# A mixture-of-experts layer on one core: the first tiles' table moved ahead of other TensorE work, and weight columns gathered a step earlier

## The chip, the cores and the metric

The kernel runs on one core of a Trainium2 chip. A core has five engines that run side by side, each with its own instruction queue in program order: PE (TensorE, matmuls and transposes; its weight loads are listed as PEld), DVE (VectorE), ACT (ScalarE), POOL (GpSimd, which here issues the indirect transfers) and SP (SyncE, which issues plain transfers). They wait for each other through semaphores. Transfers run on DMA engines beside them. The metric is the device time of one execution in microseconds (us), the median of several runs; lower is better.

## The reference

4096 tokens of 256 values, 64 groups of 64 tokens. A gate picks two of eight experts for each token; each expert is a network of three layers (256 to 512 to 512 to 256). The two experts' outputs are weighted by the gate's softmax and added to the token.

```python
var = jnp.mean(x * x, axis=-1, keepdims=True)
xn = rms_w * (x * jax.lax.rsqrt(var + EPS))
gate = xn @ wg_W + wg_b + (genre_embed @ gg_W + gg_b)
gate_w = jax.nn.softmax(gate, axis=-1)
topk_w, topk_i = jax.lax.top_k(gate_w, TOP_K)          # TOP_K = 2
cw = jnp.sum(jax.nn.one_hot(topk_i, E, dtype=x.dtype) * topk_w[..., None], axis=-2)
h1 = jax.nn.relu(jnp.einsum('bsh,ehm->bsem', x, W1) + b1)
h2 = jax.nn.relu(jnp.einsum('bsem,emn->bsen', h1, W2) + b2)
out_e = jnp.einsum('bsen,enh->bseh', h2, W3) + b3
x = x + jnp.einsum('bseh,bse->bsh', out_e, cw)
```

## The kernel before

Only the chosen experts are computed. Tokens are sorted by expert into tiles of 128 rows (`BT`), each of one expert, and 67 such tiles run in this profile. The first eight (`E`) are special: the first 1024 tokens (`NA = 8` columns of 128, "part A") are routed ahead of the rest, and each expert gets one tile of them, so that matmuls can begin while the other 3072 tokens ("part B") are still being routed.

**The head.** `first_part` loads x, transposes it on PE (`turn`, L184: four transposes of a block into one PSUM bank and one copy to SBUF, on ACT or DVE), multiplies the transposed blocks with the gate weights (`gates`, L194, gates lie in rows of 32 per block), and turns the gates upright again (`upright`, L205: one ACT copy and four transposes). `squares` (L177) sums the squares of one column of tokens on ACT or DVE. For part A, `choose` (L252) finds the two largest gates: for each of the two, a maximum (L271), a compare (L275), and then a product with `rank`, a maximum and a compare (L277, L279, L281) that keep the first among equal gates. `count` (L287) makes running counts of the tokens of each expert, `totals` (L300) sums over partitions with four small matmuls on PE, `pick` (L306) gives each token its place in its expert's tile, a compare (L406) makes a one-hot of the places, and 16 matmuls (L424) turn the one-hot into a table of token numbers, from which L426 and L427 make `idxA`, the row numbers that POOL gathers by. `busy` (L214) puts transposes of the identity on PE as filler. In this part the code stands in a `manual_schedule` block: every engine executes in program order.

**The tiles.** `gather(b)` (L587) fetches the 128 token rows of tile b by an indirect transfer on POOL; `gather_cw(b)` (L591) fetches the rows of gate weights ("weight columns") of those tokens in the same way, into a ring `cg` of three buffers. `transpose_x(b)` (L606) brings the rows into matmul layout: for tiles under 12 with PE transposes (L618) and a DVE copy (L620), later through a DRAM scratch and a DVE transpose (L609). `stage_1`, `stage_2` and `stage_3` copy the weights of the tile's expert on DVE into fixed places (L646, L654, L665) for tiles from 8 on; `stage_3` also copies the expert's weight column out of `cg` (L668) and scales the bias with it (L670). `layer1`, `layer2`, `layer3` are the matmuls (L680, L693, L705) with ReLU on ACT (L683, L696). At the end DVE forms `y` (L706) and POOL adds it to the output with an indirect accumulating transfer (L707); each add waits for the one before it. For tiles under 8, L670 and L706 read `cg` itself and not a copy.

**The order.** A step s runs layer 1 of tile s, layer 2 of tile s-1 and layer 3 of tile s-2. `head_step` (tiles 0 to 6) lays pieces of the routing of part B (`rest`, L457 on) between the matmuls, by budgets in ns that `routing` and the generator's `yield`s count. Steps 8 to 59 stand outside of `manual_schedule`: there a planner orders each engine's instructions by when their inputs would be ready. The last steps and the tail (one of 14 branches, by how many tiles there are) are in program order again. Weights of all experts (16 MB) are loaded by SP behind x, in the order of the experts, until about 65 us.

Of the kernel before, what the change touches and what calls it, by code (L numbers as in the profile page):

```python
# [9 lines left out]
F32 = mybir.dt.float32  # L10
# [3 lines left out]
ALU = mybir.AluOpType  # L14
# [7 lines left out]
def kernel(  # L22
# [31 lines left out]
    NA = 8  # L54
# [59 lines left out]
    make_identity(nc, ident)  # L114
    ones = const.tile([P, P], F32, name="ones")
    nc.gpsimd.memset(ones, 1.0)
    rank = const.tile([P, E], F32, name="rank")
    nc.gpsimd.iota(rank, [[-1, E]], base=E, channel_multiplier=0, allow_small_or_imprecise_dtypes=True)
    tri = const.tile([P, P], F32, name="tri")
    nc.gpsimd.affine_select(  # L120
        out=tri, in_=ones, pattern=[[1, P]], compare_op=ALU.is_gt, fill=0.0, base=0, channel_multiplier=-1
# [4 lines left out]
    segA = const.tile([P, E, NA], F32, name="segA")  # L126
    nc.gpsimd.memset(segA, 1.0)
    nc.gpsimd.memset(segA[:, :, 0:1], 0.0)
    iotx = const.tile([P, P, GC], F16, name="iotx")
    nc.gpsimd.iota(iotx, [[1, P], [0, GC]], base=0, channel_multiplier=0, allow_small_or_imprecise_dtypes=True)  # L130
    iot = const.tile([P, NREST], F32, name="iot")
# [25 lines left out]
    def t2(name, n, dt=F32):  # L157
        return buf(gx, [P, n], name, dt)
# [18 lines left out]
    def squares(i, eng):  # L177
        xi = xin[i // TPB][:, i % TPB, :]
        if eng == "A":
            nc.scalar.activation(sqs[eng], xi, AF.Square, accum_out=ss[:, i : i + 1])  # L180
        else:
            V.tensor_tensor_reduce(sqs[eng], xi, xi, 1.0, 0.0, ALU.mult, ALU.add, ss[:, i : i + 1])

    def turn(j, c, n, eng):  # L184

        tp, xTc = TB[n], hid[:, n].rearrange("p c t -> p (c t)")
        for k in range(TPB):
            nc.tensor.transpose(tp[:, ts(k, P)], xin[j][:, k, ts(c, P)], ident)
        if eng == "V":
            V.tensor_copy(xTc, tp)  # L190
        else:
            nc.scalar.copy(xTc, tp)

    def gates(c, bufs, bank=PB[3]):  # L194

        for q, n in enumerate(bufs):
            nc.tensor.matmul(
                bank[32 * q : 32 * q + 32, :],
                lhsT=wg_sb[:, c, :],
                rhs=hid[:, n].rearrange("p c t -> p (c t)"),  # L200
                start=(c == 0),
                stop=(c == HC - 1),
            )

    def upright(nq, bank=PB[3], dst=PB[4]):  # L205

        R = 32 * nq
        nc.scalar.copy(gTs[0:R, :], bank[0:R, :])
        gtp = dst[:, 0 : TPB * R].rearrange("p (k r) -> p k r", k=TPB)
        for k in range(TPB):  # L210
            nc.tensor.transpose(gtp[:, k], gTs[0:R, ts(k, P)], ident[0:R, 0:R])
        return gtp.rearrange("p k (q e) -> p q k e", q=nq)[:, :, :, 0:E]

    def busy(n):  # L214

        for _ in range(n):
            nc.tensor.transpose(PB[6][:, 256 : 256 + P], ident, ident)

    class Part:


        def __init__(self, z, i0, i1):
            self.i0, self.i1, self.n, self.z = i0, i1, i1 - i0, z
            n = self.n
            self.t = {a: t2(f"{a}{z}", n) for a in ("var", "root", "y", "t", "rstd", "m1", "m2", "top", "den", "d2")}
            self.gate, self.w = t3(f"gate{z}", n), t3(f"w{z}", n)
            self.oh, self.pr = (buf(gx, [P, TOPK, n, E], f"{a}{z}") for a in ("oh", "pr"))
            self.inc = buf(gx, [P, E, n], f"inc{z}")
            self.seg = segA if z == "A" else seg
            self.off = PB[6][:, 448 : 448 + 2 * E].rearrange("p (a e) -> p a e", a=2)  # L230
            self.cw8 = cw8B[:, i0:i1, :] if z == "B" else t3("cw8A", n)
# [19 lines left out]

        def choose(self, raw):  # L252

            m1, m2, top = (self.t[a] for a in ("m1", "m2", "top"))
            gate, left, rstd = self.gate, self.pr[:, 0], self.t["rstd"]
            if raw is None:
                V.tensor_tensor(gate, graw[:, self.i0 : self.i1, :], self.over_e(rstd), ALU.mult)
            else:
                q = raw.shape[1]
                V.tensor_tensor(  # L260
                    gate.rearrange("p (q k) e -> p q k e", q=q),
                    raw,
                    self.over_e(rstd).rearrange("p (q k) e -> p q k e", q=q),
                    ALU.mult,
                )
            yield
            V.tensor_tensor(gate, gate, self.over_i(ggate), ALU.add)
            yield
            for k, (g, m) in enumerate(((gate, m1), (left, m2))):
                sc = self.oh[:, k]  # L270
                V.tensor_reduce(m, g, AX.X, ALU.max)  # L271
                yield
                if k == 0:
                    nc.gpsimd.tensor_tensor(self.w, gate, self.over_e(m1), ALU.subtract)
                V.tensor_tensor(sc, g, self.over_e(m), ALU.is_equal)  # L275
                yield
                V.tensor_tensor(sc, sc, self.over_i(rank), ALU.mult)  # L277
                yield
                V.tensor_reduce(top, sc, AX.X, ALU.max)  # L279
                yield  # L280
                V.tensor_tensor(sc, sc, self.over_e(top), ALU.is_equal)  # L281
                yield
                if k == 0:
                    V.scalar_tensor_tensor(left, sc, -BIG, gate, ALU.mult, ALU.add)
                    yield
# [58 lines left out]
    def first_part():  # L344
# [25 lines left out]
        for i in range(TPB):  # L370
            squares(TPB + i, "VVAA"[i])
        V.tensor_copy(ggate, gps)
        gates(0, (0, 2))
        gates(1, (1, 3))
        pA.root()
        pA.norm()
        raw = upright(GA)
# [9 lines left out]
            load_weights(e)  # L387


        for q in range(4):  # L390
            turn(GA + q, 0, q, "A")
        gates(0, range(4))
        squares(NA, "A")
        squares(NA + 1, "A")
        for _ in pA.choose(raw):
            pass
        pA.count()
        for q in range(2):
            turn(GA + q, 1, q, "A")
        pA.totals()  # L400
        slot = pA.gate
        V.scalar_tensor_tensor(
            slot, pA.inc.rearrange("p e i -> p i e"), -1.0, pA.over_i(pA.off[:, 0, :]), ALU.add, ALU.add
        )
        pA.pick(lo16A.rearrange("p (k i) -> p k i", k=TOPK), slot)
        V.tensor_tensor(ohA, iotx, lo16A.unsqueeze(1).to_broadcast([P, P, GC]), ALU.is_equal)  # L406
        V.tensor_tensor(
            mvA.rearrange("p (k i) e -> p k i e", k=TOPK),
            pA.oh,
            toka.unsqueeze(1).unsqueeze(3).to_broadcast([P, TOPK, NA, E]),  # L410
            ALU.mult,
        )
        V.tensor_copy(totA, pA.off[:, 1, :])
        for q in range(2, 4):
            turn(GA + q, 1, q, "A")
        squares(NA + 2, "A")
        gates(1, range(4))
        raw = upright(4)
        nc.scalar.copy(graw[:, NA : NA + 4 * TPB, :].rearrange("p (q k) e -> p q k e", q=4), raw)
        squares(NA + 3, "A")  # L420
        squares(NA + 4, "A")
        tabA = PB[7][:, 0:E]
        for g in range(GC):
            nc.tensor.matmul(tabA, lhsT=ohA[:, :, g], rhs=mvA[:, g, :], start=(g == 0), stop=(g == GC - 1))  # L424

        V.tensor_scalar(sa[:, 0:E], tabA, 0.0, float(NT), ALU.is_equal, ALU.mult)  # L426
        V.scalar_tensor_tensor(idxA, tabA, float(OFFA), sa[:, 0:E], ALU.add, ALU.add)  # L427

    def second_part():

        j0 = GA + 4
        for i in range(NA + 8, NI - 4):
            squares(i, "V")
        for c in range(HC):
            for q in range(2):
                turn(j0 + q, c, 2 * c + q, "A")
        for c in range(HC):
            gates(c, (2 * c, 2 * c + 1), PB[7])
        busy(4)
        raw = upright(2, PB[7], PB[6])  # L440
        busy(2)
        nc.scalar.copy(graw[:, j0 * TPB : NI, :].rearrange("p (q k) e -> p q k e", q=2), raw)
        vps = PB[6][:, 384 : 384 + 2 * E * MC]
        nc.tensor.transpose(vps, vecs, ident[: 2 * E * MC, : 2 * E * MC])
        V.tensor_copy(vT.rearrange("p l e c -> p (l e c)"), vps)
        for i in range(NA + 5, NA + 8):
            squares(i, "A")

    mms = []

# [310 lines left out]
    def step(s, last):  # L761
# [26 lines left out]
        if not ends:  # L788
            layer3(s - 2)
            if s < last:  # L790
                stage_3(s - 1)
        if s < last:
            gather_cw(s)

    SURE = E + NSURE
    CUT = SURE - 2
# [5 lines left out]
    V.tensor_copy(tok16, tokv)  # L802

    with tc.manual_schedule():
        first_part()
        for b in range(3):
            gather(b)
        second_part()
        for i in range(NI - 4, NI):
            squares(i, "V")  # L810
        other = rest()

        def routing(ns):
            while ns > 0:
                c = next(other, None)
                if c is None:
                    break
                ns -= c

        busy(18)  # L820
        routing(100)
        stage_1(0)
        transpose_x(0)
        for s in range(E - 1):
            head_step(s, routing)
        for _ in other:
            pass
        step(E - 1, SURE)
# [59 lines left out]
```

## Time and profile before

| | us |
|---|---|
| median of 3 runs | 530.45 (530.05 to 531.66) |
| the profiled execution | 530.45 |
| its span, first to last instruction | 528.6 |
| PE busy in the span | 510.9 (97%) |
| DVE, ACT, POOL busy | 285.5, 215.4, 282.1 |
| mean granted TensorE clock | 0.993 |
| first layer-1 matmul (tile 0) | at 32.03 |
| layer 1 of tile 1 | at 34.85 |
| from layer 1 of one tile to the next, from tile 12 on | 7.09 |

Times in the profile count from the first instruction. The execution's time is 1.85 us longer than the span. A row of the timeline gives start, duration, engine, line of the kernel, operation, and tiles as out<-in; in brackets stands how long the engine was idle before, and what the profile takes for the release. Names have lost their buffer numbers, so that all `cg` look alike. A busy PE is not PE at its peak[...].

### The profile page before, as it was taken

How to read it: one execution, taken by the hardware profiler on the slowest of the kernel's cores; microseconds unless marked ns; L12 is line 12 of the kernel's file. 1: busy time of each engine (PE TensorE's matmuls, PEld its weight loads, DVE VectorE, ACT ScalarE, POOL GpSimd, SP SyncE). 2: the span in 40 equal slices, each digit the busy share in tenths (PEclk: the TensorE clock that was granted, in tenths of full speed). 3: DMA queues.
4: the chain of work that ended last, by engine and by line, in shares of the span. 5: the costliest groups of instructions: out<-in, count | busy, mean ns of one | idle time of the engine just before them, and what ended most of it. 6: DMA issues, size and time to landing. Idle time of an engine off the chain costs nothing. (4 is left out here: it accounts for less than half of the span.)

```text
span 528.6 us, 11667 instructions
## 1 busy us (share of the span) xinstructions
PE 510.9 (97%) x4026; PEld 487.6 (92%) x4026; DVE 285.5 (54%) x651; ACT 215.4 (41%) x588; POOL 282.1 (53%) x237
## 2 busy tenths in 40 slices
PE   8989999989999999999999999999999999999992
PEld 6579999979999999999999999999999999999991
DVE  4686973347555555555555555555555555545540
ACT  3754334433443444444334444443444444344430
POOL 4132678677875555555555555555555553245441
PEclk9999999999999999999999999999999999999997
DMA  8999976335444333334333332334333323323211
GB/s 262 385 397 377 373 203 181 70 89 104 97 86 82 68 72 75 71 74 76 78 72 79 70 75 66 80 72 82 71 72 76 73 66 51 52 35 75 29 22 22
DMA packets 67230, 58.92 MB, mean 111 GB/s; under 512 B 38721, under 2 KB 58130, under 8 KB 66900
## 3 DMA queue, kind: packets, MB, share of 16 engines
q1 hardware_dynamic: 51312, 40.69, 24.2%
q0 software_dynamic: 15136, 17.32, 20.1%
q8 instruction: 34, 0.56, 0.4%
q14 instruction: 40, 0.33, 0.2%
q10 hardware_dynamic: 708, 0.03, 0.1%
HBM read 42.54 MB, written 20.45 MB: 119 GB/s over the span
## 5 line engine op out<-in xcount | busy, mean ns | idle before, releaser
L693 PE MATMUL pb<-hid,big 128*128 128x128 f32 x1888 | 220.6, 275 | 0.1
L693 PEld LDWEIGHTS pb<-hid,big 128*128 128x128 f32 x1888 | 215.7, 192 | 0.4 <-ACT hid L683 0.3
L707 POOL DMA_INDIRECT out_dram<-y,idxR x59 | 107.9, 1830 | 150.5 <-DVE y L706 143.8
L654 DVE COPY big<-w2a 128x2048 f32 x59 | 72.6, 1230 | 131.5 <-PE pb L693 87.1
L696 ACT ACTIVATE hid<-pb,bb 128x128 f32<-128x128 f32 x236 | 86.9, 368 | 128.4 <-PE pb L693 92.4
L683 ACT ACTIVATE hid<-pb,bb 128x128 f32<-128x128 f32 x236 | 86.5, 368 | 123.5 <-PE pb L680 101.4
L680 PEld LDWEIGHTS pb<-xTb,big 128*128 128x128 f32 x944 | 114.6, 192 | 3.2 <-issue 0.2
L680 PE MATMUL pb<-xTb,big 128*128 128x128 f32 x944 | 114.9, 275 | 0.0
L705 PE MATMUL pb<-big,hid 128*128 128x256 f32 x472 | 111.7, 380 | 2.8 <-DVE big L665 2.8
L705 PEld LDWEIGHTS pb<-big,hid 128*128 128x128 f32 x472 | 85.2, 190 | 12.1 <-DVE big L665 3.0
L578 POOL DMA_INDIRECT cg<-cwdR,idxR x59 | 65.2, 1105 | 19.8 <-DVE xTb L609 12.2
L578 POOL DMA_INDIRECT xg<-in_x_dram,idxR x59 | 63.7, 1079 | 21.8 <-issue 16.2
L646 DVE COPY big<-w1a 128x1024 f32 x59 | 44.3, 751 | 19.6 <-PE pb L680 13.4
L706 DVE SCALAR_TENSOR_TENSOR y<-pb,cw,bc 128x256 f32<-128x256 f32 x59 | 28.5, 483 | 31.0 <-PE pb L705 30.9
L665 DVE COPY big<-w3a 128x1024 f32 x59 | 40.3, 683 | 0.0
L693 PE MATMUL pb<-hid,w2a 128*128 128x128 f32 x256 | 29.9, 275 | 0.0
L693 PEld LDWEIGHTS pb<-hid,w2a 128*128 128x128 f32 x256 | 29.3, 192 | 0.0
L609 DVE STREAM_TRANSPOSE xTb<-gTs 128x256 f32<-128x256 f32 x55 | 23.6, 429 | 3.6 <-issue 3.6
L707 POOL DMA_INDIRECT out_dram<-y,idxA x8 | 13.7, 1716 | 15.3 <-DVE sli L506 7.0
L670 DVE TENSOR_SCALAR bc<-b_sb,cw 128x256 f32 x59 | 20.9, 354 | 0.4
L696 ACT ACTIVATE hid<-pb,vT 128x128 f32<-128x128 f32 x32 | 11.3, 368 | 19.7 <-PE pb L693 19.2
L578 POOL DMA_INDIRECT xg<-in_x_dram,idxA x8 | 10.1, 1266 | 15.8 <-DVE idxA L427 9.6
(185 smaller groups left out, 265.5 us busy)
## 6 DMA issues: line engine op xcount, KB each, us to landing
w2a<-in_L_cond_W_dram SPq DMA_DIRECT2D x8, 1024.0 KB
scr<-xg SPq DMA_DIRECT2D x55, 128.0 KB
gTs<-scr SPq DMA_DIRECT2D x220, 32.0 KB
big<-in_x_dram SPq DMA_DIRECT2D x8, 512.0 KB
w1a<-in_L_cond_W_dram SPq DMA_DIRECT2D x8, 512.0 KB
w3a<-in_L_cond_W_dram SPq DMA_DIRECT2D x8, 512.0 KB
out_dram<-in_x_dram SPq DMA_DIRECT2D x4, 768.0 KB
out_dram<-in_x_dram SPq DMA_DIRECT2D x1, 1024.0 KB
```

The source lines that it names most:

```text
L578: nc.gpsimd.indirect_dma_start(out=dst, out_offset=None, in_=src, in_offset=bass.IndirectOffsetOnAxis(ap=index(b), axis=0), bounds_check=N ...
L609: V.transpose(xTb.rearrange("p c (k b) -> p k c b", b=SQ), shs[:, b % 2].rearrange("p k (a c) -> p k c a", a=SQ),)
L646: V.tensor_copy(w1, w1a[:, e].rearrange("p e c m -> p (e c) m"))
L654: V.tensor_copy(w2, w2a[:, ex[b]].rearrange("p e c m -> p (e c) m"))
L665: V.tensor_copy(w3, w3a[:, e].rearrange("p e c m -> p (e c) m"))
L680: nc.tensor.matmul(ph, lhsT=w1[:, c, ts(m, P)], rhs=xTb[:, c, :], start=(c == 0), stop=(c == HC - 1))
L683: nc.scalar.activation(h1[:, m, :], ph, AF.Relu, bias=bb[:, 0, m : m + 1])
L693: nc.tensor.matmul(ph, lhsT=w2[:, m, ts(n, P)], rhs=h1[:, m, :], start=(m == 0), stop=(m == MC - 1))
L696: nc.scalar.activation(h2[:, n, :], ph, AF.Relu, bias=bb[:, 1, n : n + 1])
L705: nc.tensor.matmul(po, lhsT=h2[:, n, :], rhs=w3[:, n, :], start=(n == 0), stop=(n == MC - 1))
L706: V.scalar_tensor_tensor(y, po, cw, bc, ALU.mult, ALU.add)
L707: add = nc.gpsimd.indirect_dma_start(out=orows, out_offset=bass.IndirectOffsetOnAxis(ap=index(b), axis=0), in_=y, in_offset=None, bounds_c ...
```

## The change

- `rank` and its iota go; a constant `segT` (ones with a zero at the head of each group of eight) comes. In `choose`, the three operations product, maximum and compare become a scan that numbers the equal gates and one operation that keeps number 1.
- In `first_part` the gates of the first two blocks run block by block (both halves of the first, then both of the second) and no longer by halves. Squares are spread over the part in groups (`some`). `totals` and the product `mvA` come before the second half's transposes of the next four blocks, and all four of these stand together behind it. The compare is cut in two halves of eight columns, each followed by its eight table matmuls, and these come before `gates(1)` and `upright(4)`. `totA` is copied at the end.
- In `second_part` the first two transposes of the last blocks, `upright(4)` and the transpose of the biases come first, the DVE squares are 10 and then 4, one filler group of 4 goes and one of 2 stays; `transpose_x(0)`, the transposes of tile 0's rows, stands before the last `upright`. The 18 fillers before the routing go.
- In `step`, `gather_cw(s + 1)` takes the place of `gather_cw(s)`; at step 7 both are issued.

```diff
-    rank = const.tile([P, E], F32, name="rank")
-    nc.gpsimd.iota(rank, [[-1, E]], base=E, channel_multiplier=0, allow_small_or_imprecise_dtypes=True)
+    segT = const.tile([P, NB, E], F32, name="segT")
+    nc.gpsimd.memset(segT, 1.0)
+    nc.gpsimd.memset(segT[:, :, 0:1], 0.0)
...
-                V.tensor_tensor(sc, sc, self.over_i(rank), ALU.mult)
+                V.tensor_tensor_scan(
+                    nth.rearrange("p i e -> p (i e)"),
+                    segT[:, 0 : self.n].rearrange("p i e -> p (i e)"),
+                    sc.rearrange("p i e -> p (i e)"), 0.0, ALU.mult, ALU.add,
+                )
                 yield
-                V.tensor_reduce(top, sc, AX.X, ALU.max)
-                yield
-                V.tensor_tensor(sc, sc, self.over_e(top), ALU.is_equal)
+                V.scalar_tensor_tensor(sc, nth, 1.0, sc, ALU.is_equal, ALU.mult)
...
-        gates(0, (0, 2))
-        gates(1, (1, 3))
+        for q in range(GA):
+            for c in range(HC):
+                gates(c, (2 * q + c,), q0=q)
...
+        some(2)
         for q in range(4):
             turn(GA + q, 0, q, "A")
         gates(0, range(4))
-        squares(NA, "A")
-        squares(NA + 1, "A")
+        some(2)
         for _ in pA.choose(raw):
             pass
         pA.count()
-        for q in range(2):
-            turn(GA + q, 1, q, "A")
         pA.totals()
+        V.tensor_tensor(mvA..., pA.oh, toka..., ALU.mult)
+        for q in range(4):
+            turn(GA + q, 1, q, "A")
         slot = pA.gate
         V.scalar_tensor_tensor(slot, ...)
         pA.pick(lo16A..., slot)
-        V.tensor_tensor(ohA, iotx, lo16A..., ALU.is_equal)
-        V.tensor_tensor(mvA..., pA.oh, toka..., ALU.mult)
-        V.tensor_copy(totA, pA.off[:, 1, :])
-        for q in range(2, 4):
-            turn(GA + q, 1, q, "A")
-        squares(NA + 2, "A")
-        gates(1, range(4))
-        raw = upright(4)
-        nc.scalar.copy(graw..., raw)
-        squares(NA + 3, "A")
-        squares(NA + 4, "A")
         tabA = PB[7][:, 0:E]
-        for g in range(GC):
-            nc.tensor.matmul(tabA, lhsT=ohA[:, :, g], rhs=mvA[:, g, :], start=(g == 0), stop=(g == GC - 1))
+        GH = GC // 2
+        for g0 in range(0, GC, GH):
+            hs = slice(g0, g0 + GH)
+            V.tensor_tensor(ohA[:, :, hs], iotx[:, :, hs], lo16A[:, hs]..., ALU.is_equal)
+            for g in range(g0, g0 + GH):
+                nc.tensor.matmul(tabA, lhsT=ohA[:, :, g], rhs=mvA[:, g, :], start=(g == 0), stop=(g == GC - 1))
+        some(3)
+        gates(1, range(4))
 
         V.tensor_scalar(sa[:, 0:E], tabA, 0.0, float(NT), ALU.is_equal, ALU.mult)
         V.scalar_tensor_tensor(idxA, tabA, float(OFFA), sa[:, 0:E], ALU.add, ALU.add)
+        V.tensor_copy(totA, pA.off[:, 1, :])
...
-    def second_part():
+    def second_part(some):
         j0 = GA + 4
-        for i in range(NA + 8, NI - 4):
+        nc.scalar.copy(gTs, PB[3])
+        for q in range(2):
+            turn_pe(j0 + q, 0, q)
+        raw = upright(4, copied=True)
+        vps = PB[6][:, 384 : 384 + 2 * E * MC]
+        nc.tensor.transpose(vps, vecs, ident...)
+        for i in range(NA + 10, NI - 4):
+            if i == NI - 8:
+                V.tensor_copy(vT..., vps)
             squares(i, "V")
-        for c in range(HC):
-            for q in range(2):
-                turn(j0 + q, c, 2 * c + q, "A")
+        for q in range(2):
+            turn_copy(q, "A")
+        nc.scalar.copy(graw[:, NA : NA + 4 * TPB, :]..., raw)
+        for q in range(2):
+            turn(j0 + q, 1, 2 + q, "A")
+        some(3)
         for c in range(HC):
             gates(c, (2 * c, 2 * c + 1), PB[7])
-        busy(4)
+        busy(2)
+        for i in range(NI - 4, NI):
+            squares(i, "V")
+        transpose_x(0)
         raw = upright(2, PB[7], PB[6])
-        busy(2)
         nc.scalar.copy(graw[:, j0 * TPB : NI, :]..., raw)
-        vps = ...
-        nc.tensor.transpose(vps, vecs, ident...)
-        V.tensor_copy(vT..., vps)
-        for i in range(NA + 5, NA + 8):
-            squares(i, "A")
...
-        if s < last:
+        if s == E - 1:
             gather_cw(s)
+        if s + 1 < max(last, SURE):
+            gather_cw(s + 1)
...
-        for i in range(NI - 4, NI):
-            squares(i, "V")
         other = rest()
...
-        busy(18)
         routing(100)
         stage_1(0)
-        transpose_x(0)
```

## The prediction

> **What bounds the kernel now.** I read the page's engine line first, then busy time by stretches, then the order of time around the stretches that are not full, then who waits for whom.
>
> ```profile
> PE 510.9 (97%) x4026; PEld 487.6 (92%) x4026; DVE 285.5 (54%) x651; ACT 215.4 (41%) x588; POOL 282.1 (53%) x237
> ...
> 26.70:32.03 5.33, 4.11 (x31) 3.23 (x32) 4.56 (x23) 3.14 (x10) 0.97 (x2) 1.00 1.01 399
> 32.03:116.30 84.27, 83.71 (x706) 81.59 (x706) 50.03 (x115) 34.34 (x96) 51.37 (x46) 1.00 0.75 235
> 116.30:119.30 3.00, 0.24 (x3) 0.05 (x1) 2.44 (x6) 0.37 (x1) 2.23 (x2) 1.00 0.27 85
> 119.30:503.90 384.60, 384.51 (x3031) 373.02 (x3032) 208.86 (x433) 158.63 (x432) 209.72 (x156) 1.00 0.36 71
> ```
>
> Columns: stretch, length, then busy time of PE, PEld, DVE, ACT, POOL, granted clock, DMA share, GB/s. From the first layer-1 matmul (32.03) to 503.9, PE is full but for 0.6 us in all and one hole of 3 us at 116.3; tiles follow each other every 7.09 us. A shorter wait of DVE, ACT or POOL there buys nothing. What can move the end is when tile 0 starts, the hole, and a new hole. The tail (503.9 on) follows PE: the last y ends at 518.96, and its add starts 0.45 later.
>
> The head, in order of time (start, duration, engine, line):
>
> ```profile
> 17.42 0.30 PEld L303 LDWEIGHTS pb<-incA,tri 128*128 128x128 f32 x2
> ...
> 19.09 1.22 DVE L406 TENSOR_TENSOR hotA<-iotx,lo16A 128x2048 f16<-128x2048 f16 x1
> ...
> 21.80 1.12 PEld L424 LDWEIGHTS <-hotA 128*128 128x128 f16 x16
> ...
> 23.25 0.17 DVE L427 SCALAR_TENSOR_TENSOR idxA<-pb,sa 128x8 int32<-128x8 f32 x1
> ...
> 23.69 1.12 POOL L578 DMA_INDIRECT xg<-in_x_dram,idxA  x1 [9.61 <-DVE idxA L427]
> ...
> 29.09 1.95 PEld L217 LDWEIGHTS pb<-ident 128*128 128x128 f32 x18 [0.46 <-DVE vT L445]
> ...
> 31.00 0.32 PEld L618 LDWEIGHTS pb<-ident,xg 128*128 128x128 f32 x2
> ...
> 31.34 1.28 ACT L314 ACT_TABLE_LOAD   x1
> ...
> 32.03 1.86 PEld L680 LDWEIGHTS pb<-xTb,w1a 128*128 128x128 f32 x16 [0.71 <-DVE xTb L620]
> ...
> 33.52 0.30 DVE L323 TENSOR_TENSOR d2A<-d2A,denA 128x8 f32<-128x8 f32 x1
> ...
> 34.85 1.86 PEld L680 LDWEIGHTS pb<-xTb,w1a 128*128 128x128 f32 x16 [0.72 <-ACT hid L683]
> ```
>
> The compare that feeds the table (L406) is done at 20.31, but its matmuls start at 21.80: ahead of them on PE stand gates and the upright transposes, which waited for ACT. The gather follows idxA. The trace's record of its semaphore is full at 30.57, 6.88 us after the gather's start (6.05 and 6.17 for the next two); the transposes of tile 0 start at 31.00, just as the 18 fillers end. So landing and fillers decide tile 0 together.
>
> **The change, step by step.**
>
> (1) *First tiles' gates, buffer by buffer.* Before, the group took 2.67 us from 9.09 with a wait for the buffer loaded third; the same eight passes take 1.95 at 14.72. Up to 0.3 us sooner: ACT's copy, which waited 0.36, starts 0.28 earlier, and so does choosing.
>
> (2) *Scan in place of rank, maximum and compare.* Per k three operations at 0.26 apart (0.77) become a scan (L291: 0.29, plus 0.03) and one operation of 0.26: 0.19 less, 0.38 for both. The counting scan then ends at 16.89-0.28-0.38 = 16.2.
>
> (3) *Totals ahead of the c=1 transposes.* They queue behind gates(0), whose matmuls end at 16.67, so they load at about 16.6 instead of 17.42: slot (18.13) starts at 17.3. mvA (0.28) is made in that wait. Slot and pick take 0.95, as before: lo16A at 18.25.
>
> (4) *Compare in two halves, table at once.* No row shows 1024 elements. A line through L522 (2048 in 1.22) and L524 (1104 in 0.72) gives 0.68 each, my value, 1.39 together with the gap; the other end is twice 1.22. The second half is done at 19.64. Its eight matmuls (0.07 each) run to 20.4; the 16 transposes put ahead of the table fill 17.2 to 18.95 on PE and the first half's matmuls the rest. sa at 20.45, **idxA at 20.65 instead of 23.25: 2.6 us**; gather at 21.1.
>
> (5) *Landing.* [...] 6.88 while the weights stream (399 GB/s in the stretch above). [...] by the row they land at **28.0**. I take the row, since the weights stream as thickly at 21; the range is 5.5 to 7.5.
>
> (6) *What has to be done by then.* PE: gates(1) to 22.4, eight transposes, upright (0.42), vecs, eight transposes (0.87 each eight), last gates behind their ACT copies to 26.7, two fillers: 27. DVE: 14 squares at 0.47 plus totA and vT from 20.8: 27.8. ACT: 10 squares at 0.57, most of them in its waits. All are just under 28.0, so the moved squares, transposes and vT cost nothing; without that cover each microsecond of them would count. Of 24 fillers behind the first part 22 go: 2.4 us of PE at 0.108, which buys nothing by itself because the landing decides.
>
> (7) *transpose_x(0) ahead of upright and of the routing.* L618 28.1, copy (0.42) to 29.07, layer 1 at 29.15 (32.03 before: 2.9 sooner), the last upright hidden under the copy. But varB now stands behind that copy on DVE. Behind varB come ACT's root, the table load (1.28) and two exps, then tile 0's ReLU (2.0 after varB) and DVE's weights (over 2.94 after varB, L323), and only then tile 1's xTb copy. So tile 1's layer 1 comes 3.4 after tile 0's instead of 2.82: **32.6 instead of 34.85, 2.25 us sooner**. Behind it PE is full, the routing's DVE work hangs on PE's totals and moves along, and the weights have landed long before use.
>
> (8) *gather_cw one step earlier.* In the last steps and the tail, where code order is program order, DVE waited 0.69 us for a column, with nothing of PE behind it: 0. In tiles 8 to 59 the planner orders. The hole is there:
>
> ```profile
> 114.45 1.04 POOL L578 DMA_INDIRECT cg<-cwdR,idxR  x1 [0.30 <-issue]
> ...
> 116.86 0.15 DVE L668 COPY cw<-cg 128x1 f32 x1 [5.97 <-DMA cg<-cwdR,idxR]
> ...
> 118.59 0.68 DVE L665 COPY big<-w3a 128x1024 f32 x1
> ...
> 119.33 1.59 PEld L705 LDWEIGHTS pb<-big,hid 128*128 128x128 f32 x8 [2.98 <-DVE big L665]
> ```
>
> The late column is tile 10's. Its buffer is tile 7's, which y of tile 7 reads until 108.98; on POOL two token gathers and an add were served first. The earlier place in the code does not lift the wait for y, and POOL's rows show gathers issued well out of code order already, as their buffers came free. I take 0; the ends are -3.0 (hole gone) and +3.2 (one more add, 1.9 with its gap, and one more gather, 1.3, ahead of the column).
>
> POOL's constants (a memset of about 0.35 for an iota of 0.13) lie before 6.5, and POOL is idle until 13.77.
>
> Sum: 528.6 - 2.25 = 526.35 of span, plus the 1.85 that this execution (530.45) has around it: **528.2 us**; the execution equals the median of the runs.
>
> [...] The row 26.70:32.03 had 5.3 us of hardly anything but transposes at clock 1.00. I count nothing.
>
> **Rivals.** *A, the hole goes too*: the planner serves tile 10's column first. For it: the gather took 2.4 us, the wait was 5.97. Against: the buffer. 528.2-2.9 = 525.3. *B, the gather lands no sooner*: the 1 MB fill issued at 18.12 and the weights queued ahead set the landing, or the halves cost 1.22 each. For it: the first gather took longest. Against: the fourth and fifth gathers (31.79 and 35.81) took 6.3 and 6.5 without that fill. Time 530. *C, slower*: the planner puts tile 10's or 11's column one add and one gather later; DVE waits before a w3 copy, and PE before L705. Price 3.2: 531.4; it decides from 2.25 us of new hole on. For it: one such hole exists. Against: the order follows readiness, which is unchanged.
>
> **How the numbers follow.** Forecast 0.54, A 0.17, B 0.17, C 0.12. The likeliest alone spans 527.1 to 529.4 (landing, halves). 0.3% (1.6 us) is about what a measurement here can tell from none. Faster: 0.45 of the forecast's 0.54, all of A, a little of B: 0.64. Same: the rest of the forecast and most of B: 0.23. Slower: C and an end of B: 0.13. Range 524.9 to 530.9: it takes in A and B and leaves out C.
>
> **What would show it.** idxA near 20.7, first L578 near 21.1, L618 near 28.1, L680 near 29.15 and 32.6; the table load between them; the hole before L705 of about 3 us still near 114 to 117; steps of 7.09 after it; clock 1.00. I would be wrong if L618 starts before 27 or after 29, if tile 1's layer 1 doesn't wait for DVE, if the hole is gone or doubled, or if the steps stretch past 7.13.

## The result, and the profile after

The changed kernel takes **529.16 us** (median of 22 runs, 526.86 to 531.07); the kernel before, run beside it, takes 531.68 us (22 runs, 529.66 to 533.92). The ratio is **0.9957, 95% interval 0.9941 to 0.9972**: 0.43% faster. The prediction, 528.2 from 530.45, was 0.42%. The sum is right by luck: the lead at layer 1 is 1 us larger than it said, and nearly as much is lost behind it, so the traces are worth a closer look. The profiled execution of the changed kernel took 529.26 us, its span is 527.5, its mean clock 0.990.

First the busy time of the changed kernel by stretches, in the columns of the prediction (stretch, length, busy time of PE, PEld, DVE, ACT, POOL, granted clock, DMA share, GB/s):

```profile
24.00:28.27 4.27, 3.73 (x16) 1.14 (x15) 3.98 (x20) 3.12 (x10) 1.09 (x2) 1.00 1.06 409
28.27:113.30 85.03, 83.98 (x708) 81.64 (x706) 50.16 (x114) 35.20 (x98) 51.61 (x46) 1.00 0.76 250
113.30:116.50 3.20, 0.23 (x3) 0.03 (x1) 2.44 (x6) 0.37 (x1) 2.20 (x2) 1.00 0.18 50
116.50:119.00 2.50, 2.47 (x8) 2.04 (x9) 2.45 (x6) 0.00 (x0) 2.18 (x2) 0.66 0.26 71
119.00:121.70 2.70, 2.70 (x18) 2.61 (x16) 1.45 (x4) 0.81 (x3) 2.11 (x2) 0.69 0.59 146
121.70:503.00 381.30, 381.02 (x3010) 369.74 (x3009) 204.71 (x423) 157.52 (x430) 205.95 (x154) 1.00 0.36 70
```

Layer 1 starts at 28.27 instead of 32.03. PE is full behind it but for the one hole, which is still there, 3.20 us long instead of 2.98. New are the two rows behind it: the granted clock is 0.66 and 0.69. The trace's record of the clock has one stretch at half speed ahead of the tail, 3.41 us from 117.29 on; in the profiled execution of before that record stays at full speed from the first matmuls to the tail.

The head of the changed kernel in order of time:

```profile
16.61 0.30 PEld L317 LDWEIGHTS pb<-incA,tri 128*128 128x128 f32 x2 [0.84 <-issue]
...
18.27 1.29 DVE L437 TENSOR_TENSOR hotA<-iotx,lo16A 128x1024 f16<-128x1024 f16 x2
...
19.01 1.18 PEld L441 LDWEIGHTS <-hotA 128*128 128x128 f16 x16 [0.23 <-DVE hotA L437]
...
20.52 0.17 DVE L446 SCALAR_TENSOR_TENSOR idxA<-pb,sa 128x8 int32<-128x8 f32 x1
...
20.96 1.11 POOL L607 DMA_INDIRECT xg<-in_x_dram,idxA  x1 [6.92 <-DVE totA L447]
...
27.09 0.32 PEld L647 LDWEIGHTS pb<-ident,xg 128*128 128x128 f32 x2
...
27.71 0.42 DVE L649 COPY xTb<-pb 128x256 f32<-128x256 f32 x1
...
28.27 1.86 PEld L709 LDWEIGHTS pb<-xTb,w1a 128*128 128x128 f32 x16
...
28.73 1.28 ACT L328 ACT_TABLE_LOAD   x1
...
31.58 1.86 PEld L709 LDWEIGHTS pb<-xTb,w1a 128*128 128x128 f32 x16 [1.21 <-ACT hid L712]
```

Totals load at 16.61 (17.42 before), the table's matmuls at 19.01 (21.80), idxA follows at 20.52 (23.25), the gather at 20.96 (23.69). Tile 0's layer 1 is 3.76 us sooner, tile 1's, behind which PE is full, 3.27 us.

Where did the 3.27 go, when this pair of executions differs by only 1.19? From the starts of layer 1, tile by tile: the step from tile 10 to 11 took 7.74 instead of 7.45 (+0.29), 11 to 12 took 11.08 instead of 10.03 and 12 to 13 took 7.92 instead of 7.09 (+1.88 for the hole and the half clock: 1.7 us for 3.41 us at half speed, 0.22 for the longer hole), and the step across the switch to the last steps 7.64 instead of 7.41 (+0.23, whose cause was not looked for). That leaves 0.91 us at the last tile's layer 1 (503.04 instead of 503.95). The 1.7 us are paid by this one execution and not by the profiled one of before; how often each kernel pays them is counted below.

The hole itself, on PE, DVE and POOL of the changed kernel:

```profile
107.71 0.17 DVE L676 COPY bb<-vT 128x8 f32 x1
...
111.43 1.04 POOL L607 DMA_INDIRECT cg<-cwdR,idxR  x1 [0.30 <-issue]
...
114.06 0.15 DVE L697 COPY cw<-cg 128x1 f32 x1 [6.19 <-issue]
114.18 1.23 DVE L683 COPY big<-w2a 128x2048 f32 x1
...
115.40 0.48 DVE L735 SCALAR_TENSOR_TENSOR y<-pb,cw,bc 128x256 f32<-128x256 f32 x1
115.79 0.68 DVE L694 COPY big<-w3a 128x1024 f32 x1
...
116.53 2.36 PEld L734 LDWEIGHTS pb<-big,hid 128*128 128x128 f32 x8 [3.20 <-DVE big L694]
```

It is the same chain as before, 2.8 us earlier: DVE stands 6.2 us at the copy of tile 10's weight column, whose gather starts at 111.43; behind it in DVE's order lie the copy of a layer-2 matrix, tile 8's y and tile 9's third-layer weights, and only these release PE. PE's row shows the half clock too: eight loads take 2.36 us instead of 1.59.

### The profile page after: what moved, and what is told of

Its sections match the earlier page's. It is cut to its first block, busy times and chain, and to the rows that moved or that the text cites. A ratio compares the mean times of both kernels' runs of the same rounds, so it can differ in the third digit from the quotient of the medians.

```text
span 527.5 us, 11625 instructions
## 1 busy us (share of the span) xinstructions
PE 509.8 (97%) x4004; PEld 486.1 (92%) x4004; DVE 284.0 (54%) x644; ACT 215.9 (41%) x592; POOL 281.8 (53%) x238
## 3 DMA queue, kind: packets, MB, share of 16 engines
q0 software_dynamic: 15136, 17.32, 20.6%
## 5 line engine op out<-in xcount | busy, mean ns | idle before, releaser
L734 PE MATMUL pb<-big,hid 128*128 128x256 f32 x472 | 112.9, 383 | 3.0 <-DVE big L694 3.0
L607 POOL DMA_INDIRECT xg<-in_x_dram,idxR x59 | 62.5, 1059 | 21.0 <-issue 15.6
L638 DVE STREAM_TRANSPOSE xTb<-gTs 128x256 f32<-128x256 f32 x55 | 23.5, 428 | 3.8 <-DMA gTs<-scr 3.5
L709 PE MATMUL pb<-xTb,w1a 128*128 128x128 f32 x128 | 15.8, 276 | 1.0 <-ACT hid L712 1.0
```

Of the source, the lines that this page charges most:

```text
L607: nc.gpsimd.indirect_dma_start(out=dst, out_offset=None, in_=src, in_offset=bass.IndirectOffsetOnAxis(ap=index(b), axis=0), bounds_check=N ...
L638: V.transpose(xTb.rearrange("p c (k b) -> p k c b", b=SQ), shs[:, b % 2].rearrange("p k (a c) -> p k c a", a=SQ),)
L709: nc.tensor.matmul(ph, lhsT=w1[:, c, ts(m, P)], rhs=xTb[:, c, :], start=(c == 0), stop=(c == HC - 1))
L734: nc.tensor.matmul(po, lhsT=h2[:, n, :], rhs=w3[:, n, :], start=(n == 0), stop=(n == MC - 1))
```

## The experiments

Two theories stood against each other. **Theory**: the table's place on PE brings the lead at layer 1; the lead reaches the end, but for what hole and half clock take, in executions of both kernels. **Rival**: the lead is lost in the queue that serves the tiles behind the routing (GpSimd's gathers and adds), and the gain comes from elsewhere, as from the earlier column gather.

### The column gather alone, and the change without it

The changed kernel with `gather_cw(s)` back in step s:

```
-        if s == E - 1:
-            gather_cw(s)
-        if s + 1 < max(last, SURE):
-            gather_cw(s + 1)
+        if s < last:
+            gather_cw(s)
```

> The changed kernel with one part undone: the weight columns of tile s are gathered in step s again, not in step s-1. Theory (step 8 of the prediction: this move is worth nothing): first layer 1 at 28.3 us as in the changed kernel, the hole of about 3 us near 116 stays, time within 1 us of the changed kernel (about 529, 2.5 us below the kernel before). Rival (the columns' earlier gather carries part of the 2.5 us): slower than the changed kernel by 1 us or more, the hole longer than 3.2 us.

And the kernel before with the opposite edit:

> The kernel before with only the gather of the weight columns one step earlier. Theory: within 1 us of the kernel before (531.7), its first layer 1 at 32.0 us, its hole at 116 as it was (2.98 us). Rival (the move alone is worth something, or costs something): a difference above 1 us, with the hole shorter or longer by as much.

Without the move: 528.55 us, ratio to the kernel before 0.9950 (0.9929 to 0.9970), against 0.9957 for the whole change. The hole is there, 3.10 us long, with no half clock behind it in the profiled execution. The move alone: 532.52 us, ratio 1.0007 (0.9993 to 1.0021). It is worth nothing, and the order on POOL around the hole is the same with and without it.

### The table put back behind gates and upright

```
-            for g in range(g0, g0 + GH):
-                nc.tensor.matmul(tabA, lhsT=ohA[:, :, g], ...)
         some(3)
         gates(1, range(4))
+        nc.scalar.copy(gTs, PB[3])
+        raw = upright(4, copied=True)
+        for g in range(GC):
+            nc.tensor.matmul(tabA, lhsT=ohA[:, :, g], ...)
```

> The changed kernel with the 16 multiplications of the first tiles' table put back behind the second half of the gates and their transposes (totals stay ahead, the compare stays in halves, the scan stays). Theory (step 4: the table's place carries nearly all of the lead): idxA at 23.5 us instead of 20.5, first gather at 23.9, first layer 1 at 31.3 instead of 28.3, and the time is 3 us above the changed kernel, about that of the kernel before (531.5 to 532). Rival (transposing tile 0 first, or the scan, carries the gain): first layer 1 at or below 30, time at most 1.5 us above the changed kernel.

The table's rows of this kernel:

```profile
22.23 1.10 PE L445 MATMUL pb<-mvA,hotA 128*128 128x8 f16 x16
...
23.57 0.17 DVE L448 SCALAR_TENSOR_TENSOR idxA<-pb,sa 128x8 int32<-128x8 f32 x1
...
30.11 0.50 PE L647 MATMUL pb<-ident,xg 128*128 128x128 f32 x2 [2.41 <-DMA xg<-in_x_dram,idxA]
...
31.20 2.05 PE L709 MATMUL pb<-xTb,w1a 128*128 128x128 f32 x16 [0.20 <-DVE xTb L649]
```

idxA is at 23.57 (expected 23.5), layer 1 at 31.20 (31.3). The time is 532.69 us, ratio 1.0017 (1.0001 to 1.0032): the whole gain is gone, with scan, totals, halves and tile 0's early transposes all still in place. The table's place on PE carries the gain. PE now waits 2.41 us in plain sight, since 18 fillers no longer stand there.

### Scan undone, and tile 0's transposes put back

The changed kernel with rank, maximum and compare in place of the running sum:

```
-                V.tensor_tensor_scan(nth..., segT..., sc..., 0.0, ALU.mult, ALU.add)
-                V.scalar_tensor_tensor(sc, nth, 1.0, sc, ALU.is_equal, ALU.mult)
+                V.tensor_tensor(sc, sc, self.over_i(rank), ALU.mult)
+                V.tensor_reduce(top, sc, AX.X, ALU.max)
+                V.tensor_tensor(sc, sc, self.over_e(top), ALU.is_equal)
```

> The changed kernel with the first of equal gates found again by rank, maximum and compare in place of the running sum. Theory (step 2): everything from the count on is 0.4 us later: count's scan at 16.6, idxA at 20.9, first layer 1 at 28.65, tile 1's at 31.95; 0.4 us of time, less than a few executions can show. Rival (the running sum is worth nothing, something else on VectorE or TensorE decides): first layer 1 still at 28.3.

In one execution (529.96 us): count's scan starts at 16.54 (16.18 in the changed kernel), idxA at 20.85, layer 1 of tile 0 at 28.86: the scan is worth its 0.4. Tile 1 came at 33.18 instead of 31.95, for a reason that was not expected: layer 1 of tile 0 takes 3.37 us instead of 2.05, as at a lower clock, and the mean clock of this execution is 0.987. In front of it PE had stood idle for 1.26 us, waiting for the gather.

The changed kernel with `transpose_x(0)` behind `upright` and `routing(100)`:

```
-        transpose_x(0)
         raw = upright(2, PB[7], PB[6])
...
         routing(100)
         stage_1(0)
+        transpose_x(0)
```

> The changed kernel with tile 0's transposes and copy behind the last gates' transposes and behind the variance of the later tiles, as in the kernel before. Theory (step 7: tile 0 gains by going first, and tile 1 doesn't, since ScalarE's table load and exponentials hold its hidden layer): layer 1 of tile 0 at 29.2 instead of 28.3, that of tile 1 at 31.6 to 31.9 as in the changed kernel, so at most 0.3 us of the time. Rival (the early transposes carry the lead): tile 1's layer 1 at 32.5 or later.

```profile
21.03 0.17 DVE L446 SCALAR_TENSOR_TENSOR idxA<-pb,sa 128x8 int32<-128x8 f32 x1
...
27.80 0.18 DVE L248 TENSOR_SCALAR varB<-ss 128x24 f32<-128x24 f32 x1
...
28.25 1.28 ACT L328 ACT_TABLE_LOAD   x1
...
28.57 2.05 PE L708 MATMUL pb<-xTb,w1a 128*128 128x128 f32 x16 [0.52 <-DVE xTb L648]
...
31.42 1.80 PE L708 MATMUL pb<-xTb,w1a 128*128 128x128 f32 x14 [0.56 <-ACT hid L711]
```

In this one execution (528.77 us) idxA is 0.51 late (the scan that counts started 0.53 late already, ahead of the edit). Yet tile 1's layer 1 starts at 31.42, sooner than the 31.58 of the changed kernel: with varB ahead of tile 0's copy the table load starts at 28.25 instead of 28.73, and tile 1 follows tile 0 after 2.85 us instead of 3.31. The early transposes are worth nothing at tile 1, perhaps a little less than nothing.

### A quiet landing

The changed kernel with all weights but expert 0's, and the fill, held back:

```
         load_weights(0)
-        load_weights(1)
-        ...
...
         transpose_x(0)
+        V.memset(w1a[:, 1, 0, 0:1], 0.0)
+        load_weights(1)
+        ...
```

> The changed kernel with all weight loads but those of expert 0, and the first copy of x to the output, held back until tile 0's transposed copy is done (a one-column memset on VectorE in front of them), so that the first gather of rows meets no streaming weights. Theory (the 6.1 us from first gather to landing come from the weight stream, which fills the DMA engines from 9 to 30 us): the landing takes 2.5 to 3.5 us, at 23.5-24.5; layer 1 of tile 0 starts no sooner all the same (28.0-28.3), held by the fourteen squares on VectorE to 27.7. Rival (the 6 us are the gather's own path): landing still at 27. The later tiles wait for their weights; the whole time says nothing.

Busy time between 21.00 and 27.60, first of the changed kernel:

```profile
21.00:27.60 6.60, 6.35 (x37) 3.21 (x33) 5.80 (x29) 5.05 (x15) 3.08 (x3) 1.00 1.05 405
```

then of the quiet one:

```profile
21.00:27.60 6.60, 5.90 (x41) 3.55 (x37) 6.18 (x33) 5.24 (x16) 4.08 (x4) 1.00 0.23 70
```

With 70 GB/s instead of 405 in flight, the first four gathers, of which the first started at 21.00, took **3.0 us in the median** from issue to landing; the first of the changed kernel took 6.1 (20.96 to 27.05). So the transfers beside it make the landing long; the edit holds weights and fill back together, so it does not tell the two apart. And layer 1 of tile 0 starts at 27.61, only 0.66 sooner, although by these numbers its rows are there some 3 us sooner: the squares on DVE end at 27.1, and the copy follows. (The later tiles then wait for their weights, so this execution's 535.3 us say nothing.)

### Six buffers for the gathered columns

```
-        cg = cgs[b] = ring(run, [P, E], "cg", 3, b)
+        cg = cgs[b] = ring(run, [P, E], "cg", 6, b)
```

> The changed kernel with six buffers for gathered weight columns in place of three, so that tile 10's gather no longer has to wait for tile 7's output. Theory (the lead of 3.3 us at layer 1 reaches the end, and the changed kernel loses it partly to the hole at 116 and to a spell of half clock behind it): the hole of 3.2 us goes, no clock below 1.00 near 117-121, and the time falls by 3 us (hole alone) to 5 us (with the spell, 1.7) below the changed kernel, to 524-526. Rival (the work behind the routing is tied to the GpSimd queue and the routing's end, whose time the change hardly moved): another wait takes the hole's place within two tiles, and the time falls by less than 1.5 us.

> The kernel before with six buffers for gathered weight columns. Theory: its hole of 2.98 us goes, 531.7 becomes 527-529; the changed kernel with six buffers is 3.3 us below this one, since nothing then eats the lead of 3.3 us at layer 1. Rival (the lead is absorbed behind the routing, whatever the hole): the two kernels with six buffers lie within 1.5 us of each other.

The theory of the remedy failed. On the changed kernel: 529.51 us, ratio 0.9968 (0.9944 to 0.9993), no better than without. The one hole became several waits:

```profile
99.87 1.59 PEld L734 LDWEIGHTS pb<-w3a,hid 128*128 128x128 f32 x8 [1.28 <-DVE y L735]
...
110.31 0.52 PEld L709 LDWEIGHTS pb<-xTb,big 128*128 128x128 f32 x4 [0.87 <-ACT hid L725]
...
112.57 0.52 PEld L709 LDWEIGHTS pb<-xTb,big 128*128 128x128 f32 x4 [0.93 <-issue]
...
132.03 1.59 PEld L734 LDWEIGHTS pb<-big,hid 128*128 128x128 f32 x8 [0.86 <-DVE big L694]
```

The steps that were stretched (8.67, 9.69, 8.03) carry 4.9 us over the 7.1 to 7.3 of the others. On the kernel before it is worse than nothing: 537.92 us, ratio 1.0106 (1.0075 to 1.0137), with a hole of 5.27 us at tile 11's third layer. The planner, free to gather columns earlier, serves them ahead of token rows: on POOL two columns stand at 87.83 and 89.20, where two row gathers stood (87.84 and 89.22), and these now start at 93.80 and 95.11. The rows stay late, until DVE waits 8.61 us for a tile's rows (`gTs<-scr`). Since both kernels are changed in the order of their queues by this edit, it says nothing on where the lead goes.

### Work put into the hole

Six matmuls that read tile 10's hidden layer and write an unused bank, ahead of tile 9's third layer:

```
         po = PB[5][:, 0:H]
+        if b == 9:
+            for n in range(6):
+                nc.tensor.matmul(PB[6][:, 256 : 256 + P], lhsT=ident, rhs=h2s[b + 1][:, 2, :], start=True, stop=True)
```

> The changed kernel with six matrix multiplications (identity times the third part of tile 10's hidden layer, to an unused bank) put on TensorE ahead of tile 9's third layer, that is into the hole of 3.2 us near 113-116; 1.4 us of work that depends on nothing in the hole. Theory (a spell of half clock is set off when TensorE stands idle about 3.2 us at one go; it costs 1.7 us each time, and about three of four executions of the changed kernel have one or more): the hole's idle stretch falls below 2.2 us, no half clock behind it, mean clock 0.993 or more in nearly all executions, the time 1.5 us below the changed kernel, about 527.2 (4.5 below the kernel before). Rival (the low clocks come from elsewhere, not from this hole): mean clocks spread over 0.987 to 0.996 as in the changed kernel, and the time stays at 529.

> The kernel before with the same six matrix multiplications ahead of tile 9's third layer. Theory: the kernel before has the spell as often as the changed one (its own executions show clocks of 0.987 to 0.996), so it gains as much: 1.5 to 2 us, to about 530.5, and the difference to the changed kernel with the filler is the lead at layer 1, 3.3 us. Rival (the hole of 2.98 us is too short for the spell, the low clocks come from elsewhere): no gain, 532.

PE of the changed kernel with the filler:

```profile
113.10 1.42 PEld L735 LDWEIGHTS pb<-hid,ident 128*128 128x128 f32 x12
116.10 1.59 PEld L737 LDWEIGHTS pb<-big,hid 128*128 128x128 f32 x8 [1.58 <-DVE big L694]
```

PE still can't go on before 116.10, but it stands idle for 1.58 us at one go instead of 3.20, and the eight loads behind it take 1.59. **527.67 us**, ratio 0.9919 (0.9893 to 0.9944): work that computes nothing makes the changed kernel 1.5 us faster by the medians, 2.0 by the ratios. On the kernel before: 530.72 us, ratio 0.9979 (0.9967 to 0.9991), 1.3 us.

The mean clock of the executions shows what was bought. A stretch of 3.41 us at half speed lowers the mean of such a span by 0.003. The profile of the changed kernel runs at half speed in the tail, from 520.06 on, 2.5 us after the last matmul, and that of before from 521.26 on, 2.8 us after; this takes 0.007 from the mean, so that 0.993 or more is taken for an execution with no such stretch inside. The two profiled executions agree: before, with none, has 0.993, the changed kernel, with one, 0.990. Of the twelve other profiled executions eight have 0.993 to 0.995, one 0.990 and three 0.986 to 0.988. Of the kernel before 16 of 43 have 0.993 or more, with the filler 21 of 22; of the changed kernel 6 of 22, with the filler 4 of 6.

| mean clock | before: executions, mean span | changed: executions, mean span |
|---|---|---|
| 0.993 and more | 16, 528.80 | 6, 525.67 |
| 0.989 to 0.992 | 21, 530.57 | 10, 527.34 |
| 0.988 and less | 6, 532.05 | 6, 529.08 |

Each line down costs about 1.7 us, one stretch at half speed, and **along each line the changed kernel is 3.0 to 3.2 us ahead**: the lead at layer 1 is kept, nearly whole. The 43 executions were not taken beside the 22 (the medians of before in the four sets of runs lie between 531.68 and 532.44), but the filler in both kernels, taken side by side, gives the same without any sorting: 530.72 and 527.67, 3.05 us apart. Without it the medians differ by less (2.5) because more of the changed kernel's executions lie in the last line. The rival falls.

### One buffer for the copied column

`cw` is the column's copy that y reads. With one buffer, the planner can't put tile 10's copy ahead of tile 9's y:

```
-            cw = ring(run, [P, 1], "cw", 3, b)
+            cw = ring(run, [P, 1], "cw", 1, b)
```

> The changed kernel with one buffer in place of three for the copied weight column, so that VectorE copies a tile's column only behind the output of the tile before, and tile 10's column no longer stands ahead of tile 9's third-layer weights on VectorE. No multiplication is added. Theory (the hole of 3.2 us is VectorE's place in its own queue behind a gather that lands late, not the gather itself): the wait of 6.2 us at the column's copy goes, the hole falls below 1 us and no spell of half clock follows; 2 to 3 us sooner by the hole and 1.5 by the spell, 524.5 to 526. Rival (as with six buffers, another wait of the GpSimd queue takes its place within two or three tiles): 527 to 529.

> The same with two buffers for the copied weight column: tile 10's column stands behind tile 8's output and tile 9's weights on VectorE, but ahead of tile 12's first-layer weights. Theory: the hole before tile 9's third layer goes; a shorter wait of about 1 us comes before tile 12's layer 1, since its weights' copy still stands behind the column; about 1 us above the kernel with one buffer, 525.5 to 527. Rival as for one buffer: 527 to 529.

Who waits on DVE from 104 to 122 (us in total, times, longest), in the changed kernel:

```profile
DVE cw L697 <- DMA cg<-cwdR,idxR: 7.3, 1, 7.3
DVE cw L697 <- issue: 6.2, 1, 6.2
...
```

and with one buffer:

```profile
DVE xTb L638 <- DMA gTs<-scr: 2.5, 1, 2.5
DVE big L683 <- PE pb L722: 1.7, 1, 1.7
...
```

Its busy time by stretches:

```profile
104.00:124.00 20.00, 20.00 (x159) 19.38 (x159) 7.68 (x17) 8.43 (x23) 11.11 (x10) 1.00 0.34 81
124.00:497.50 373.50, 373.24 (x2948) 362.16 (x2947) 208.79 (x425) 154.25 (x421) 208.72 (x155) 1.00 0.37 72
```

PE is full for all of the 20 us, with the clock at 1.00. **524.02 us** (523.66 to 525.49), half a us under what was expected, ratio to the kernel before **0.9864** (0.9835 to 0.9892), against 0.9957 for the change: with one digit altered the gain is three times as large. It is the fastest kernel of this case. Tile 10's column is gathered no sooner (at 112.47 instead of 111.43), but nothing that PE waits for stands behind its copy. With two buffers the wait moves, as expected, to tile 12's layer 1, which PE reaches 1.66 us too early: 526.87 us, ratio 0.9902 (0.9876 to 0.9929). In the profiled execution PE waited 1.81 us for the first gather's rows, until 28.43, and layer 1 of tile 0 started only at 29.52.

One buffer on the kernel before was not run.

## Why the prediction was right, and where its terms were off

**(1) Gates buffer by buffer: wrong, small.** 0.28 us was expected. The group takes 2.67 us from 9.06 as it took 2.67 from 9.09, and ACT's copy is 0.03 sooner.

**(2) Scan: right.** From the gates' scaling to the count's scan it takes 3.29 us instead of 3.67: 0.38, as worked out. Undone, the scan is 0.36 later.

**(3), (4) Totals ahead, halves, table: right.** 16.61 and 17.32 for totals and slot (16.6, 17.3), 1.29 for both halves (1.39), idxA at 20.52 (20.65). Taken back alone, the table's place costs 3.2 us at the end by the ratios (1.0017 against 0.9957); that is the edit that made the kernel faster.

**(5) Landing: the term that was mis-sized.** "Landing 28.0" took 6.88 us from the one row of before. It was 6.1 here (landed at 27.05); the first three gathers took 6.3 in the median in the kernel before with the filler, and 6.0 with the table put back. The range of 5.5 to 7.5 holds these. Only with the weights held back was it as short as 3.0: the row was the right choice.

**(6) What has to be done by then: right, and now level with the landing.** DVE's last square ends at 27.65 (27.8 was the number), the copy follows at 27.71. With rows at 27.05 and their transposes done at 27.60, landing and squares end within 0.1 us of each other; the quiet run shows how far tile 0 moves when only the squares are left, 0.66. Together with (5) this put tile 0 at 28.27 instead of 29.15. "22 fillers buy nothing by themselves" holds for the time on PE; what their absence does to the clock at the head is taken up at the end.

**(7) Tile 0 first: the gap was right, the worth was not asked.** Tile 1 follows after 3.31 us (3.4), so the lead is 3.27 instead of 2.25: 0.88 of the difference is tile 0's. The profile names ACT as the release of tile 1's layer 1, but DVE's copy of its rows ended last, at 31.51, as forecast. But put back, in the one execution there is, tile 1 starts no later. I had shown that varB behind the copy costs tile 1 what tile 0 gains, and had not drawn the conclusion that this part of the edit is worth nothing.

**(8) The column gather: right.** 0 by both runs. The hole stays, for the reason given.

**The clock: the step that failed.** "I count nothing", and clock 1.00 as a sign, were argued for the head, where no half clock shows in this profile (clock 1.00 from 24.00 to 28.27). But the hole I left at its 2.98 us, without asking what it does to the clock. The changed kernel's is 3.20, and in 16 of 22 executions the clock fell somewhere; the median pays one stretch, 1.7 us. Since the executions of before pay it nearly as often (27 of 43), the difference suffers less: by the lines of the table 1.0 stretch per execution against 0.77, an estimated 0.4 us. Of the lead of 3.27 that leaves 2.2 by the profiled pair (which loses 0.66 beside its stretch: the step before the hole, the hole, the switch) and 2.7 by the lines of the table (3.1 less 0.4). Measured were 2.3 (ratio) to 2.5 (medians), where the sum said 2.25: it was met because the lead was 1.0 us too small in it and the loss behind it nearly as much.

**Rivals.** A (hole goes too) did not come about by the change, and its assumption that serving the column first is enough fails too: six buffers did that and won nothing. B and C did not happen.

## What to carry to other kernels

When PE idles, look not only at the transfer that is late but at what stands behind its reader in an in-order queue. Here a copy of one column, needed only by its own tile's output (at 127.31, 13 us after the copy), held back weights that were needed at once. One buffer for the copy, which kept it from being moved ahead, cured it; more buffers for the gather did not. An idle stretch of about 3 us on PE cost more than its length in two of three executions here (16 of 22 and 27 of 43 had a mean clock under 0.993); where it can't be removed, matmuls that compute nothing, put in the middle of it so that less than 2 us (1.58 and 1.91) are left at one go, paid (1.5 and 1.3 us). Of this edit's many parts one carried the gain (the table's place on PE): take each part back by itself before keeping it.

## What the runs showed of the hardware

**The half clock behind the hole lasts 3.41 us.** In the changed kernel's profile the record of the clock starts at 4.65, turns to half speed at 117.29, back at 120.70, and to half speed again at 520.06, in the tail. From 4.65 to 117.29 it is 33 times 3.413 us, from 120.70 to 520.06 it is 117 times. The record of before starts at 5.84 and turns to half speed once, at 521.26: 151 times 3.413 us later.

**What PE did in the 3.41 us ahead of a change** can be read from these two traces, when they are cut in steps of 3.413 us from the record's start. The changed kernel's stretch with most of the hole and the one behind it, then the two of the kernel before that share its hole (columns as above):

```profile
113.87:117.29 3.42, 0.76 (x4) 0.68 (x5) 3.23 (x8) 0.12 (x1) 2.20 (x2) 1.00 0.25 77
117.29:120.70 3.41, 3.41 (x13) 2.96 (x12) 2.72 (x7) 0.20 (x1) 2.80 (x3) 0.50 0.38 88
...
115.07:118.48 3.41, 1.47 (x14) 1.28 (x12) 1.62 (x4) 0.89 (x3) 2.34 (x3) 1.00 0.47 108
118.48:121.90 3.42, 2.57 (x15) 2.37 (x16) 3.42 (x9) 0.10 (x1) 3.00 (x2) 1.00 0.18 50
```

PE was busy for 0.76 us of the first, and the next ran at half speed; the steps of before cut the hole in two, the emptier stretch holds 1.47 us, the other 2.57, and the clock stayed at 1.00. The half clock of the tail comes behind a stretch with 0.88 us of PE's work in the changed kernel (516.65 to 520.06) and 0.59 in the one before (517.85 to 521.26). So in these two executions 0.88 us and less were followed by half clock, 1.47 and more were not; what lies between was not shown. A hole's length alone does not decide: with `gather_cw(s)` back in step s it was 3.10 us, and in the profiled execution (mean clock 0.995) the eight loads behind it take 1.59 us. 16 of 22 executions of the changed kernel and 27 of 43 of the one before, 73% and 63%, had a mean clock under 0.993. With the filler, which left 1.58 and 1.91 us at one go, it was 2 of 6 and 1 of 22.

**What the fillers at the head are worth to the clock was not shown.** With rank in place of the scan, PE waited 1.26 us for the gather, and layer 1 of tile 0 took 3.37 us instead of 2.05; with the table put back, PE waited 2.41 us, and layer 1 behind it took 2.05, in one profiled execution each. The changed kernel with its 22 old fillers was not run.

**A gather under traffic.** The first gather of 128 rows on POOL's queue took 6.1 us from its start to its landing in the changed kernel and 6.9 in the one before, where the weights stream (405 GB/s from 21.00 to 27.60 in the changed kernel). With weights and fill held back, and 70 GB/s moved beside it, the first four took 3.0 us in the median.
